# Graph layer and expert layers on one Trainium2 core: own products added by VectorE out of PSUM, the bias by a product, another order between sort and layer 0, blocks growing by one tile

## Chip, cores, metric

The kernel runs on one core of one Trainium2 chip (trn2). The metric is the device time of one execution in microseconds (us). Lower is better.

## What is computed

Nodes: 6250 rows x of 256 values. Edges: 100,000, each with `src`, `dst` and a weight, handed over in the order of `dst`. LN is a layer norm without factors. The reference does four steps; each adds its result to x:

```python
# layer 0, graph
h = LN(x) @ weight_l
x = x + segment_sum(edge_weight * h[dst], src) + bias_l + LN(x) @ weight_r + bias_r
# layer 0, eight dense experts e, hidden width 256, all applied to all rows
n = LN(x); w = softmax(n @ Wr + br)
h = relu(bn1(n @ W1[e] + b1[e])); h = relu(bn2(h @ W2[e] + b2[e]))
x = x + sum_e w[e] * (h @ Wo[e] + bo[e])
# layer 1, graph: sums over dst, gathers of src
x = x + segment_sum(edge_weight * (LN(x) @ weight)[src], dst) + bias
# layer 1, 32 experts, hidden width 64, one of them for each row (argmax)
x = x + relu(relu(LN(x) @ W1[i] + b1[i]) @ W2[i] + b2[i])
```

## The kernel before

The nodes are 49 tiles of 128 rows (`NT`), and x stays in SBUF as `X`. An aggregation works on columns of 128 edges: GpSimd (POOL) gathers 128 rows from DRAM by an indirect DMA (`gather`, L201, 12 buffers), ScalarE (ACT) and VectorE (DVE) weight them in two parts (`weighted`: `m`, L230 and L231), VectorE makes one-hot matrices of the edges' places in the tile (`one_hots`, L222), and TensorE (PE) multiplies both into `acc` (L701 in layer 0). A tile has 18 columns in layer 0 (`EW`).

**Sort.** Layer 0 sums by `src`, but the edges come by `dst`. So the kernel sorts them on the chip, in 25 groups (`NG`) of 32 columns of 128 edges. `count_group` (from L448) counts how many edges of a group go to each tile: `hot` (L454), `four`, `mine`, the count products on TensorE (L464 to L474), `start` and `total` by ScalarE. `settle_group` (L479) carries the counts on: `ZJ` (L482), `wrap` (L484), `base_of` (L486), `full_of` (L488), and `sizes` on POOL (L489). `place_group` (L491) finds the place of each edge: `same` (L497), `picked`, `pos`, `over`, `place_b` (L521), `to` (L523), and ScalarE's `loads` (L502); 32 products `put` (L530) bring the edges there; ScalarE copies them out (`there`, L533), and five POOL operations (L535 to L539) add them into the table `Z`.

Between these stand, in each group, the layer norm and the dense products of two node tiles: `center0` (L541: statistics, `std` with a Sqrt on ScalarE, the centred `xn`) and `products0` (L559): `xn` is transposed, `nT` copied (L341), `ph` = products by [weight_l | weight_r], 512 wide (L570), ScalarE's `hs` = `ph` times 1/std (L571). Half of `hs` goes to `h0` in DRAM (L574, SP's queue); POOL adds the other half to `X` (L572) and then the bias (L573). The loop is L577 to L592. After it stand a check of the counts (L595 to L610).

**Layer 0.** `edges0` (L662) reads columns of edges (`idx`, `dl`, `w`) for the tiles of a block out of `ZJ` and `Z`: per two tiles a comparison (L671), two products (L675) and two reductions (L677), then small operations (L678 to L686). The weights are loaded by DMAs that ACT's queue issues (L638 to L649); VectorE and ScalarE make `scale` and `shift` of the batch norms (L652 to L660). A block is one to four tiles; `ramp` (L358) gives the sizes: 1, 1, 2, 3, nine times 4, 3, 3. `begin0` (L712) normalizes a block, makes its gates and adds the experts' biases; `hidden0` (L742; products L748, ScalarE L751) makes a hidden layer of one expert; `outs0` (L755; products L760, VectorE L762) multiplies by Wo and adds into `X`; `end0` (L765) writes the rows that layer 1 gathers to `h1`.

The order is written by hand in the main loop (L883 to L936): block by block, expert by expert. `aheads` (L374) plans how many columns are issued between two steps: in block b, the first 12 of 16 steps bring the columns of block b+1, the last 4 a quarter of block b+2's. `begin0` of the next block stands after expert 5. `edges0` of block b+2 stands at expert 0 of block b. `small1` (L779), `early_columns` (L809) and `missing` (L820) prepare layer 1. A scheduler of the framework (Tile) orders the instructions of each engine from this program by priorities and may bring an instruction forward; each engine then runs its own list in order.

Layer 1 (`columns1`, L236; `begin1` and what follows, experts' products L984 to L1000) is touched only in the type of `dl_c`.

## Time and profile before

| | us |
|---|---|
| median of five runs | 2898.52 (2897.63 to 2903.07) |
| profiled execution | 2898.38 |
| its span in the trace | 2896.6 |
| mean granted TensorE clock | 0.975 |
| sort: last `to` (L523) begins | 377.8 |
| first gather of layer 0 (L201) begins | 396.3 |
| first hidden product (L748) begins | 440.9 |
| blocks 1, 2, 3, 4, 5 begin (first L748) | 471.4, 521.2, 595.6, 694.4, 805.5 |
| block 7 begins | 1015.7 |
| gather 432 (the last of tile 24) begins | 1006.9 |

Busy time over the span, from the page:

| engine | us | share |
|---|---|---|
| PE | 2676.5 | 92% |
| DVE | 2012.8 | 69% |
| POOL | 1929.5 | 67% |
| PEld (weight loads, beside PE) | 1746.4 | 60% |
| ACT | 1625.3 | 56% |

A share is a mean over stages with different limits, so the stages are looked at one by one. The page also cuts the span into 40 slices and gives each engine's busy tenths in each. A row of a timeline is: start and duration in us, engine, line, operation, output<-inputs by the program's names, shapes, the number of operations joined in the row, and in brackets how long the engine stood idle before it and what released it. A row of windows is: stretch, its length, the busy time of each engine with the number of operations, then the granted TensorE clock, the DMA engines' busy share and GB/s. In a row for one source line, three durations stand for the least, the median and the longest, in ns.

The longest idle time of the costliest groups belongs to gathers and what they feed; "idle before" is followed by what ended it:

```profile
L201 POOL DMA_INDIRECT g<-h,idx x882 | 903.3, 1024 | 392.5 <-DVE m L231 175.4
```

`<-DVE m L231` means that a gather waited for its buffer, which came free when L231 had weighted the column 12 before.

### The profile page before, as it was taken

What the parts mean: (1) busy time and instruction counts of PE and PEld (TensorE: products, weight loads), DVE (VectorE), ACT (ScalarE), POOL (GpSimd) and SP (SyncE); (2) the same over time, 40 slices, a digit from 0 to 9 for tenths busy, and PEclk for the clock granted to TensorE, in tenths of its full rate; (3) what the DMA queues carried; (4) which work ended last, traced back from release to release, by engine and by line L of the source; (5) the groups of instructions that cost most, each with busy time, mean ns of one, the idle gap of its engine ahead of it and who ended that gap; (6) DMA issues with size and microseconds to landing.
All of it is one profiled execution on the core that took longest, in us unless ns stands there. A gap on an engine that the chain in (4) does not pass through costs nothing.

```text
span 2896.6 us, 37030 instructions
## 1 busy us (share of the span) xinstructions
PE 2676.5 (92%) x10336; PEld 1746.4 (60%) x10336; DVE 2012.8 (69%) x4917; ACT 1625.3 (56%) x3790; POOL 1929.5 (67%) x1932
## 2 busy tenths in 40 slices
PE   5888848889999999999999998779999999999998
PEld 2444427666566666666666665556666666666666
DVE  8999977778768767666666556666666666666630
ACT  6777737555555555555555545455555555555532
POOL 4666667777766676766675527677777777777720
PEclk9999968999999999999999999899999999999999
DMA  4000043333333333333332214333333333333310
GB/s 150 19 19 19 19 144 96 99 100 102 93 99 95 91 101 95 92 100 97 90 103 83 79 39 141 101 106 100 106 108 109 107 108 101 109 106 108 109 46 12
DMA packets 123140, 260.73 MB, mean 90 GB/s; under 512 B 32236, under 2 KB 68904, under 8 KB 122920
## 3 DMA queue, kind: packets, MB, share of 16 engines
q0 software_dynamic: 79872, 218.21, 26.4%
q1 hardware_dynamic: 31672, 32.42, 3.4%
q10 hardware_dynamic: 11376, 7.60, 0.9%
q8 instruction: 85, 1.39, 0.2%
q14 instruction: 135, 1.11, 0.1%
HBM read 238.87 MB, written 19.25 MB: 89 GB/s over the span
## 4 chain that ended last, share of the span: by engine, by line
PE 63%; DMA 8%; DVE 6%; issue 4%; ACT 3%; POOL 1%; ACTq 0%; DVEq 0%; POOLq 0%
PE ph L748 19%; PE py L760 10%; PE py L1000 9%; PE ph L984 9%; PE acc L701 6%; DMA g<-h,src_c 4%; PE acc L277 4%; DMA g<-h,idx 3%; DVE m L231 2%; ACT m L230 2%; PE ph L214 1%; POOL g L201 1%; PE ph L987 1%; PE tr L340 1%; PE pl L957 1%
## 5 line engine op out<-in xcount | busy, mean ns | idle before, releaser
L201 POOL DMA_INDIRECT g<-h,idx x882 | 903.3, 1024 | 392.5 <-DVE m L231 175.4
L201 POOL DMA_INDIRECT g<-h,src_c x718 | 728.6, 1015 | 228.8 <-issue 102.7
L230 ACT ACTIVATE m<-g,w 128x256 fp32r<-128x256 f32 x882 | 394.7, 500 | 259.6 <-PE acc L701 138.3
L751 ACT ACTIVATE hT<-ph,shift,scale 128x512 f32<-128x512 f32 (+3 forms) x480 | 329.2, 696 | 315.7 <-PE ph L748 313.9
L230 ACT ACTIVATE m<-g,val_c 128x256 fp32r<-128x256 f32 x718 | 349.3, 503 | 277.8 <-PE acc L277 132.2
L231 DVE SCALAR_TENSOR_TENSOR m<-g,val_c,m 128x256 fp32r<-128x256 f32 x718 | 336.6, 482 | 214.2 <-ACT m L230 209.7
L231 DVE SCALAR_TENSOR_TENSOR m<-g,w,m 128x256 fp32r<-128x256 f32 x882 | 397.2, 476 | 42.6 <-ACT m L230 41.9
L748 PE MATMUL ph<-nT,w 128*128 128x512 f32 (+3 forms) x960 | 373.1, 524 | 25.0 <-ACT hT L751 24.9
L760 PE MATMUL py<-wo,hT 128*128 128x256 f32 x1568 | 380.6, 386 | 15.3 <-DVE X L762 11.3
L1000 PE MATMUL py<-w,hm 128*128 128x256 f32 x1568 | 384.9, 383 | 4.1 <-ACT hm L989 4.1
L701 PE MATMUL acc<-m,s 128*128 128x512 f32 x882 | 341.5, 490 | 37.8 <-DVE scale L657 24.7
L984 PE MATMUL ph<-nT,w 128*128 128x512 f32 (+2 forms) x832 | 376.1, 573 | 0.0
L748 PE MATMUL ph<-hT,w 128*128 128x512 f32 (+3 forms) x960 | 368.2, 518 | 0.5 <-ACT hT L751 0.5
L760 PEld LDWEIGHTS py<-wo,hT 128*128 128x128 f32 x1568 | 293.4, 192 | 82.5 <-DVE X L762 27.5
L277 PE MATMUL acc<-m,s 128*128 128x512 f32 x782 | 332.1, 499 | 1.7 <-DVE m L231 1.7
L1000 PEld LDWEIGHTS py<-w,hm 128*128 128x128 f32 x1568 | 290.3, 192 | 54.2 <-ACT hm L989 6.2
L222 DVE TENSOR_TENSOR s<-col,dl 128x384 fp32r<-128x384 f32 x294 | 161.3, 551 | 186.2 <-PE acc L701 183.8
L748 PEld LDWEIGHTS ph<-nT,w 128*128 128x128 f32 x960 | 175.5, 195 | 174.1 <-issue 118.3
L989 ACT ACTIVATE hm<-ph,b 128x512 f32<-128x512 f32 (+2 forms) x208 | 136.8, 659 | 198.7 <-PE ph L987 198.3
L748 PEld LDWEIGHTS ph<-hT,w 128*128 128x128 f32 x960 | 175.8, 193 | 119.2 <-issue 88.5
L701 PEld LDWEIGHTS acc<-m,s 128*128 128x128 f32 x882 | 169.4, 195 | 109.8 <-issue 48.8
L984 PEld LDWEIGHTS ph<-nT,w 128*128 128x128 f32 x832 | 157.3, 191 | 102.0 <-issue 81.6
(248 smaller groups left out, 3358.1 us busy)
## 6 DMA issues: line engine op xcount, KB each, us to landing
g<-h,idx POOLq DMA_INDIRECT x882, 2.8
g<-h,src_c POOLq DMA_INDIRECT x718, 2.8
h<-hs SPq DMA_DIRECT2D x25, 256.0 KB, 2.1
X<-in_x_dram SPq DMA_DIRECT2D x12, 512.0 KB, 9.4
out_dram<-o SPq DMA_DIRECT2D x11, 512.0 KB, 3.4
h<-hs SPq DMA_DIRECT2D x9, 512.0 KB, 3.1
w<-in_L_ffn_W_dram ACTq DMA_DIRECT2D x2, 2048.0 KB, 11.3
wo<-in_L_ffn_Wo_dram ACTq DMA_DIRECT2D x1, 2048.0 KB, 19.9
```

Source lines behind the costliest of these rows:

```text
L201: nc.gpsimd.indirect_dma_start(out=g, out_offset=None, in_=h, in_offset=bass.IndirectOffsetOnAxis(ap=idx, axis=0))
L222: nc.vector.tensor_tensor(s[:, :n], col[:, None, :].to_broadcast([P, n, P]), dl[:, j:j + n, None].to_broadcast([P, n, P]), OP.is_equal)
L230: nc.scalar.activation(m[:, 0, :], g, AF.Copy, scale=w)
L231: nc.vector.scalar_tensor_tensor(m[:, 1, :], g, w, m[:, 0, :], op0=OP.mult, op1=OP.subtract)
L277: nc.tensor.matmul(acc, s[:, (j - js.start) % SJ, :], m, start=opens, stop=done)
L701: nc.tensor.matmul(acc, s[:, j % SJ, :], m, start=(j == 0), stop=(j == EW - 1))
L748: nc.tensor.matmul(ph[:, :nw], (w1, w2)[layer][:, e, k, m * P:(m + 1) * P], src[:, k, :nw], start=(k == 0), stop=(k == 1))
L751: nc.scalar.activation(hT[:, m, :nw], ph[:, :nw], AF.Relu, bias=shift[:, layer, c:c + 1], scale=scale[:, layer, c:c + 1])
L760: nc.tensor.matmul(py, hT[:, k, j * P:(j + 1) * P], wo[:, e, k, :], start=(k == 0), stop=(k == 1))
L984: nc.tensor.matmul(ph[:, :nw], w1f[:, k, c * P:(c + 1) * P], nT[:, k, :nw], start=(k == 0), stop=False)
L989: nc.scalar.activation(hm[:, :nw], ph[:, :nw], AF.Relu, bias=b1[:, c:c + 1])
L1000: nc.tensor.matmul(py[:, j, :], now[:, cols], w2f[:, c, :], start=False, stop=(c == NC1 - 1), skip_group_check=True)
```

## The change

1. `products0` adds the own products to `X` by one VectorE operation out of PSUM; the two POOL adds go, and `hs` is half as wide. The statistics become `stats0`, done a group earlier than `center0`.
2. The bias is cut into three bf16 pieces at the start (on POOL), and a product of 128x256 adds it into `acc` in each tile of layer 0.
3. The last group's `to` is made in two halves, its five adds to `Z` are VectorE's, and the check of the counts is issued after `to`. `tc.issue_after(x)` puts the instructions in its body behind instruction x in the scheduler's order.
4. Between the sort and layer 0, `edges0` of block 0 stands first; the loads of weights are issued by SP behind it, `edges0` of block 1 after them, that of block 2 after half of the first tile's columns. From block 1 on, `edges0` of block b+2 is behind the newest operation of `outs0`; `small1`, `early_columns` and parts of `missing` too. In block 0, the first columns stand behind the block's norm and gates.
5. The blocks of layer 0 grow as 1, 1, 1, 1, 2, 2, 2, 3, 3, 3, six times 4, 3, 3: 18 in place of 15.
6. `dl_c` is bf16.

```diff
     nc.scalar.dma_start(wlr[:, :, 1, :], a["L0_gnn_weight_r"].rearrange("(k p) d -> p k d", p=P))
-    bias0 = across("L0_gnn_bias_l", early)
-    bias0r = across("L0_gnn_bias_r", early)
+    bias0 = across("L0_gnn_bias_l", prep)
+    bias0r = across("L0_gnn_bias_r", prep)
     nc.gpsimd.tensor_add(bias0, bias0, bias0r)
+    bias0_b = const.tile([P, D], BF, name="bias0_b")
+    nc.gpsimd.memset(bias0_b, 0.0)
+    ones_b = const.tile([P, P], BF, name="ones_b")
+    nc.gpsimd.memset(ones_b, 0.0)
+    for i in range(3):
+        own = slice(32 * i, 32 * i + 1)
+        nc.gpsimd.memset(ones_b[own, :], 1.0)
+        for _ in range(i):
+            nc.gpsimd.tensor_copy(bias0_b[own, :], bias0[own, :])
+            nc.gpsimd.tensor_sub(bias0[own, :], bias0[own, :], bias0_b[own, :])
+        nc.gpsimd.tensor_copy(bias0_b[own, :], bias0[own, :])
...
-    ramp = [1, 1, 2, 3] + [NB] * 9 + [3, 3]
+    ramp = [1] * 4 + [2] * 3 + [3] * 3 + [NB] * 6 + [3, 3]
...
         to = early.tile([P, CB, P, 4], BF, tag="to", name="to", bufs=2)
-        nc.vector.tensor_tensor(to, place_b[:, :, None, :].to_broadcast([P, CB, P, 4]),
-                                which_q[:, None, :, :].to_broadcast([P, CB, P, 4]), OP.is_equal)
+        final = g == NG - 1
+        step = CB // 2 if final else CB
+        for b in range(0, CB, step):
+            bs = slice(b, b + step)
+            placed = nc.vector.tensor_tensor(to[:, bs], place_b[:, bs, None, :].to_broadcast([P, step, P, 4]),
+                                             which_q[:, None, :, :].to_broadcast([P, step, P, 4]), OP.is_equal)
...
         some = early.tile([P, 2, NT], F32, tag="some", name="some", bufs=2)
-        nc.gpsimd.tensor_add(there[:, 0], there[:, 0], there[:, 1])
...
-    def center0(tiles):
+        eng = nc.vector if final else nc.gpsimd
+        eng.tensor_add(there[:, 0], there[:, 0], there[:, 1])
...
+        return placed
+    def stats0(tiles):
...
         nc.vector.tensor_scalar(std[:, :n], mv[:, :n, 1], LN_EPS, None, op0=OP.add)
-        shift = work.tile([P, NB], F32, tag="shift", name="shift")
+        shift = work.tile([P, NB], F32, tag="shift", name="shift", bufs=3)
         nc.scalar.activation(std[:, :n], std[:, :n], AF.Sqrt)
+        return tiles, std, shift
+    def center0(tiles, std, shift):
+        n = len(tiles)
+        rstd = work.tile([P, NB], F32, tag="rstd0", name="rstd0")
+        nc.vector.reciprocal(rstd[:, :n], std[:, :n])
             nc.scalar.activation(xn[:, j, :], X[:, t, :], AF.Identity, bias=shift[:, j:j + 1])
-        return tiles, xn, std
-    def products0(tiles, xn, std):
+        return tiles, xn, rstd
+    def products0(tiles, xn, rstd):
         n = len(tiles)
-        rstd = work.tile([P, NB], F32, tag="rstd0", name="rstd0")
-        nc.vector.reciprocal(rstd[:, :n], std[:, :n])
-        hs = early.tile([P, 2, 2, D], F32, tag="hs", name="hs", bufs=2)
+        hs = early.tile([P, 2, D], F32, tag="hs", name="hs", bufs=2)
                 nc.tensor.matmul(ph, nT[:, k, :], wlr[:, k], start=(k == 0), stop=(k == 1))
-            nc.scalar.activation(hs[:, j], ph, AF.Copy, scale=rstd[:, j:j + 1])
-            nc.gpsimd.tensor_add(X[:, t, :], X[:, t, :], hs[:, j, 1, :])
-            nc.gpsimd.tensor_add(X[:, t, :], X[:, t, :], bias0)
-        nc.sync.dma_start(h0[tiles[0] * P:(tiles[0] + n) * P, :].rearrange("(t p) d -> p t d", p=P), hs[:, :n, 0, :])
+            nc.scalar.activation(hs[:, j], ph[:, 0, :], AF.Copy, scale=rstd[:, j:j + 1])
+            nc.vector.scalar_tensor_tensor(X[:, t, :], ph[:, 1, :], rstd[:, j:j + 1], X[:, t, :],
+                                           op0=OP.mult, op1=OP.add)
+        nc.sync.dma_start(h0[tiles[0] * P:(tiles[0] + n) * P, :].rearrange("(t p) d -> p t d", p=P), hs[:, :n, :])
     counted = count_group(0)
-    centered = center0(pairs[0])
+    measured = stats0(pairs[0])
+    centered = center0(*measured)
+    measured = stats0(pairs[1])
         products0(*tiles0)
-        place_group(g, *now[:2])
+        placed = place_group(g, *now[:2])
         if g + 1 < NG:
-            centered = center0(pairs[g + 1])
+            centered = center0(*measured)
+            if g + 2 < NG:
+                measured = stats0(pairs[g + 2])
...
     most = early.tile([P, 2], F32, name="most")
-    nc.vector.tensor_reduce(most[:, 0:1], sizes.rearrange("p t g -> p (t g)"), AX.X, OP.max)
...
+    with tc.issue_after(placed.ins):
+        nc.vector.tensor_reduce(most[:, 0:1], sizes.rearrange("p t g -> p (t g)"), AX.X, OP.max)
...
             tc.tile_pool(name="psum_y0", bufs=1, space=bass.MemoryType.PSUM) as psum_y:
-        wr = wp.tile([P, 2, NX0], F32, name="wr")
-        nc.scalar.dma_start(wr, a["L0_ffn_Wr"].rearrange("(k p) e -> p k e", p=P))
...
-        bn = wp.tile([P, 2, 5, 2 * NX0], F32, name="bn")
-        nc.scalar.dma_start(bn, a["bn"])
-        wo = wo_pool.tile([P, NX0, 2, D], F32, name="wo")
-        for w, name in ((w1, "L0_ffn_W1"), (w2, "L0_ffn_W2"), (wo, "L0_ffn_Wo")):
-            nc.scalar.dma_start(w.rearrange("p e k h -> p (e k) h"), a[name].rearrange("e (k p) h -> p (e k) h", p=P))
...
             dl = wp.tile([P, NB, EW], F32, tag="dl", name="dl", bufs=3)
-            nc.vector.tensor_copy(dl[:, :n], bothi[:, :n])
+            told.append(nc.vector.tensor_copy(dl[:, :n], bothi[:, :n]))
         nblk = len(blocks0)
-        edges = [edges0(blocks0[0]), edges0(blocks0[1])]
+        told = []
+        edges = [edges0(blocks0[0])]
+        behind = ExitStack()
+        behind.enter_context(tc.issue_after(told[0].ins))
+        wr = wp.tile([P, 2, NX0], F32, name="wr")
+        nc.sync.dma_start(wr, a["L0_ffn_Wr"].rearrange("(k p) e -> p k e", p=P))
+        bn = wp.tile([P, 2, 5, 2 * NX0], F32, name="bn")
+        nc.sync.dma_start(bn, a["bn"])
+        wo = wo_pool.tile([P, NX0, 2, D], F32, name="wo")
+        for w, name in ((w1, "L0_ffn_W1"), (w2, "L0_ffn_W2"), (wo, "L0_ffn_Wo")):
+            nc.sync.dma_start(w.rearrange("p e k h -> p (e k) h"), a[name].rearrange("e (k p) h -> p (e k) h", p=P))
+        bo = wp.tile([P, D], F32, name="bo")
+        nc.vector.memset(bo, 0.0)
+        nc.sync.dma_start(bo[:NX0, :], a["L0_ffn_bo"])
+        gT = wp.tile([P, NB * P], F32, name="gT")
+        nc.vector.memset(gT, 0.0)
...
+        edges.append(edges0(blocks0[1]))
+        behind.close()
...
                         nc.tensor.matmul(acc, s[:, j % SJ, :], m, start=(j == 0), stop=(j == EW - 1))
+                        if j == 0:
+                            nc.tensor.matmul(acc[:, 0, :], ones_b, bias0_b, start=False, stop=False,
+                                             skip_group_check=True)
...
         plans[-1] = [cum[-1] + (NE - tail + CS // 2 + 3) * max(0, u + 1 - head) / (2 * NX0 - head) for u in range(2 * NX0)]
+        sums.upto(cum[0] // 2)
+        with tc.issue_after(newest["rest"].ins):
+            edges.append(edges0(blocks0[2]))
+        normed = [newest[k] for k in ("xn", "nT", "gates")]
+        def columns(b, e, half):
+            with ExitStack() as behind:
+                for ins in normed if b == 0 and e < 2 else ():
+                    behind.enter_context(tc.issue_after(ins.ins))
+                sums.upto(plans[b][2 * e + half])
             for e in range(NX0):
-                if e == 0 and b + 2 < nblk:
-                    edges.append(edges0(blocks0[b + 2]))
+                if e == 0 and 0 < b < nblk - 2:
+                    with tc.issue_after(newest["out"].ins):
+                        edges.append(edges0(blocks0[b + 2]))
                 if b == nblk - 3 and e == 3:
-                    small1()
-                    early_columns()
+                    with tc.issue_after(newest["out"].ins):
+                        small1()
+                        early_columns()
                 if final and e >= 5:
-                    next(fill)
-                sums.upto(plans[b][2 * e])
+                    with tc.issue_after(newest["out"].ins):
+                        next(fill)
+                columns(b, e, 0)
```

## The prediction

> **What bounds the kernel now.** I read the 40 slices of the page first, then the busy times by stage, then timelines of one sort group, of the sort's end and of the first blocks of layer 0.
>
> ```profile
> PE   5888848889999999999999998779999999999998
> DVE  8999977778768767666666556666666666666630
> PEclk9999968999999999999999999899999999999999
> ```
>
> One digit is 72.4 us. Up to slice 5 (362 us, the sort) VectorE is the full engine; then TensorE is, except in slices 5 to 8 (the step into layer 0 and its small blocks) and around 1750 to 1900. The change touches the sort and layer 0's beginning, so these two are costed.
>
> Busy time of every engine in 50 us of the sort (columns: stretch, length, PE, PEld, DVE, ACT, POOL, clock, DMA share, GB/s):
>
> ```profile
> 150.00:200.00 50.00, 43.95 (x190) 22.17 (x191) 50.00 (x109) 41.18 (x153) 33.55 (x34) 1.00 0.07 21
> ```
>
> VectorE has no gap, TensorE has 6.05 us: 1.7 us in each group of 14.34 us (from the starts of `to`, L523: 20 groups lie between 63.55 and 350.34). Part of VectorE's time is not work. Timeline of one group (start, duration, engine, line):
>
> ```profile
> 350.34 2.27 DVE L523 TENSOR_TENSOR to<-place_b,which_q 128x4096 bf16<-128x4096 bf16 x1
> 350.55 2.66 POOL L572 TENSOR_TENSOR X<-X,hs 128x256 f32<-128x256 f32 x1 [0.50 <-ACT hs L571]
> 352.67 5.14 PE L530 MATMUL put<-loads,to 128*128 128x245 bf16 x22
> 353.28 0.73 POOL L573 TENSOR_TENSOR X<-X,L_gnn_bias_l_b 128x256 f32<-128x256 f32 x1
> 353.33 0.73 DVE L484 TENSOR_SCALAR wrap<-total 128x49 f32<-128x49 f32 x1
> 353.98 0.80 POOL L572 TENSOR_TENSOR X<-X,hs 128x256 f32<-128x256 f32 x1
> 353.98 0.20 DVE L488 SCALAR_TENSOR_TENSOR full_of<-total,full_of 128x49 f32<-128x49 f32 x1
> 354.17 0.68 DVE L486 TENSOR_TENSOR base_of<-total,wrap 128x49 bf16<-128x49 f32 x1
> ```
>
> L484, L486 and L488 have the same 49 columns; L488 takes 0.20, the other two 0.7, and each of those ends with the POOL add beside it. The POOL add is stretched likewise (2.66 beside `to`, 0.73 alone).
>
> **The change, part by part.**
>
> *Own products and bias out of POOL.* It removes the 98 POOL adds (L572, L573). Over the 25 groups the least and median durations are: L484 174 and 728 ns, L486 199 and 673, L497 398 and 877, L482 404 and 751. Taking L482 in full, the excess is 0.55 + 0.47 + 0.48 + 0.35 = 1.85 us a group; I take 1.75, because POOL keeps five adds of its own (L535 to L539) and one subtraction. Added are two `scalar_tensor_tensor` a group, 128x256, PSUM and SBUF in. The nearest row has this very shape:
>
> ```profile
> L762 DVE SCALAR_TENSOR_TENSOR X<-py,gate,X x392: 464/478/486, 450.6 to 1821.9; 128x256 f32<-128x256 f32 x196
> ```
>
> It takes 478 ns alone, and L231's six in a row took 2.46 us, 0.41 each; so +0.8 to +0.96 a group. Net on VectorE: -0.8 to -0.95 us of 14.34.
>
> [...]
>
> But VectorE's gain is only paid until TensorE and ScalarE set the period. In the group above ScalarE's `nT` (350.37) waits behind its `hs` (349.78), the four products L570 start at 350.80 and end at 352.78, and `put` starts at 352.67 while `to` had ended at 352.61. How long TensorE waits for `to` (us, times, longest), from 63 to 350 us:
>
> ```profile
> PEld L530 <- DVE to L523: 13.9, 20, 1.5
> ```
>
> That is 0.70 a group, the most that a faster VectorE takes off this wait. Following the chain `put`, `there`, two `loads`, `start`, `nT`, `nT`, products, `put` in the changed kernel's built order (its `hs` is half as wide, its Sqrt is one group earlier) I get 0.33 a group. I take the middle of the two, 0.5: 23 groups x 0.5 = **-11.5 us**; bounds 0 and 23 x 0.95 = -22.
>
> The additions also make VectorE wait for `ph`. In the built order they stand on both sides of `four` (L458 of before), right behind `hot`; queued behind them are `mine`, and so the counts, `start` and ScalarE's `loads`. `ph` was ready at 352.78, `hot` started at 354.76, so 2 us cover the wait; without them it costs what it exceeds them, on VectorE itself.
>
> *Bias in three bf16 pieces.* In the built order 11 of the new POOL operations stand before the iota of `which_t` (12.82). No row has an operation of one partition; the bounds are 0 and the 0.80 of L192's add, 0 to 8.8 us in all. Nearest in size are the adds of 49 columns (0.27 to 0.30); I take 0.4 each, 4.4 us. POOL makes `ahead` at 15.04 + 0.22, VectorE uses it at 17.25 (L439), so 2.0 us are covered: **+2.5 us**, 0 to +7.
>
> The products of 128x256 bf16 on TensorE: 49, priced by L998 (the same shape, 109 ns from start to start). The first 19 or so are in the stretch that the gathers set (below); 30 x 0.11 = **+3.3 us**.
>
> *The end of the sort, and layer 0's beginning.* After the last `place_b`:
>
> ```profile
> 376.25 0.29 DVE L521 TENSOR_TENSOR place_b<-pos,over 128x32 bf16<-128x32 f32 x1
> 376.46 1.42 DVE L596 TENSOR_REDUCE most<-sizes 128x1 f32<-128x1225 f32 x1
> 377.80 2.27 DVE L523 TENSOR_TENSOR to<-place_b,which_q 128x4096 bf16<-128x4096 bf16 x1
> 380.13 7.39 PE L530 MATMUL put<-loads,to 128*128 128x245 bf16 x32 [3.04 <-DVE to L523]
> 396.31 1.39 POOL L201 DMA_INDIRECT g<-h,idx  x1 [6.80 <-DVE at_m L827]
> ```
>
> L596 moves behind `to` (-1.4) and `to` comes in halves (-1.1). Between the last Z (389.5) and the first gather VectorE did two memsets (0.75), small operations of L785 to L827 and half of block 1's `edges0`, now all later: about -2.3. First gather about 391.5, -4.8. POOL's five Z adds on VectorE instead are equal (49 columns, 0.2 to 0.3 each).
>
> What follows is set by the gathers until TensorE has a full load. TensorE busy, by block (length, busy):
>
> ```profile
> 471.30:521.10 49.80, 38.92 (x213) 0.89 0.34 98
> 595.50:694.30 98.80, 87.17 (x323) 0.97 0.36 99
> 805.40:910.50 105.10, 105.01 (x367) 1.00 0.34 96
> ```
>
> ```profile
> 497.40:548.20 50.80, 39.81 (x36) 0.90 0.35 97
> 953.20:1006.80 53.60, 35.83 (x36) 1.00 0.32 90
> ```
>
> The second fence is POOL in line L201 alone: 36 gathers take 50 us early (1.38 each) whatever TensorE does. The smaller blocks cost TensorE nothing by their size: the pitch of L748 is 112, 216, 322 and 429 ns for one to four tiles. So the place to compare is one where both have done 19 tiles and aggregated 24 (432 gathers): before, block 7's start at 1015.7, gather 432 having left at 1006.9. After, 391.5 + 431 x 1.379 = 986. But `edges0` of block b+2 now stands behind the previous block's outs. In the built order the indices of blocks 3 and 4 (gathers 54 and 72) are written only after all 54, and after 71, earlier columns have been weighted; before, gather 72's came after 37. The queue runs dry twice, for about 8.5 and 10 us: the way from a last gather to its weighted column, and `edges0` of two tiles (L671 to L683, 5 to 7 us). 986 + 18.5 = 1004.5, and the same state is passed some 5 us later, 1009.7: **-6 us** with the -4.8 in it. Bounds: without stops -29 (nearly TensorE's own limit), with pitch 1.44 or longer stops +10.
>
> *Three more blocks* (18 for 15): three more begin0/end0, among them ACT table loads of 1.28 us. They lie beside products of the running block, which TensorE has queued. I cost them 0; uncovered, two loads a block, +7.7 us. The weights' loads on SP instead of ACT take away 8 us in which ACT issues DMAs (391.4 to 399.5), but the wait that this frees is before the first tile's gathers are in, so no more than the gathers give. `small1`, `early_columns` and `missing` move late; from 1725 to 1900 TensorE has gaps of 25 us, so 0, +-3. Layer 1 is unchanged but for `dl_c` in bf16; VectorE has slack there: 0.
>
> **Sum**, against the profiled execution's own 2898.38 (span 2896.6 and 1.8 around it; the median, 2898.52, is 0.1 from it): +2.5 - 11.5 - 6 + 3.3 = -11.7, so **2887 us**.
>
> **Rivals.**
>
> *B, VectorE is the sort's only bound and the gathers don't stop.* For: no gap in VectorE's row, and `to` ended 0.06 before `put` began. Against: the 0.33 of the chain, and the order of the columns 54 and 72. +2.5 - 22 - 29 + 3.3: 2853 us.
>
> *C, the sort keeps its period*, since `nT`, products and `put` follow each other through ScalarE. For: TensorE's 1.7 us of gaps a group are less than half waits for `to`. +2.5 + 0 - 6 + 3.3: 2898 us.
>
> *D, slower: the gather stream stops at block heads.* Place: POOL's queue at each head of blocks 3 to 8, where `edges0` waits for the previous block's outs. Two stops are counted; price 10 us each. A third brings 2897, from the fourth on it is slower: 2907 us. For: gathers are what slices 5 to 8 wait for. Against: from block 5 on, the built order has 17 or more gathers written ahead, 23 us.
>
> *E, the change doesn't free VectorE*: what remains on POOL holds L484, L486 and L497 as before, and the two additions come on top, 24 x 0.85 = +20: 2913 us.
>
> **How the numbers follow.** A difference of 0.2% (5.8 us; 2892.7 to 2904.3) is about what a measurement of this kernel can tell from none. Forecast 0.54 (its own range 2874 to 2900: faster 0.38, same 0.16); B 0.20, faster; C 0.11 (same 0.09, faster 0.02); D 0.11 (slower 0.10, same 0.01); E 0.04, slower. Faster 0.60, same 0.26, slower 0.14. The range, 2858 to 2907, leaves out the far end of B (about 0.1) and E with the worse half of D (0.1); it takes in the bounds of the sort and the gathers one at a time.
>
> **What would show it.** Period between `to`s about 13.8 us; L484 and L486 at 0.2; if they stay at 0.7, E. VectorE with gaps in the sort means that the chain is the bound; none and a period of 13.4 means B. First gather near 382. POOL idle twice near gathers 54 and 72; more often, D. The first hidden product near 420, 24 tiles aggregated near 995. TensorE in layer 0's blocks of four at 105 us plus 0.44. The forecast is wrong if layer 1 changes by more than 3 us, or if any block after the tenth has TensorE gaps.

## The result and the profile after

The changed kernel is **slower**: median 2910.91 us (2902.22 to 2915.62, 24 runs) against 2901.93 us (45 runs of the kernel before), ratio 1.0030 (1.0024 to 1.0035). A second measurement (chip number 11 on record) gave 1.0036 (1.0023 to 1.0048). The forecast was 2887, 0.4% faster, in a range of 2858 to 2907. The profiled execution took 2901.92 us (span 2900.1), 3.5 more than that of before; it is the fastest of the changed kernel's runs, and so is the traced one of the second measurement (2902.21); experiment 10 comes back to this. The medians of the kernel before differ between measurements (2896 to 2902, and far more in seven runs, experiment 11), so versions are compared by their ratio to the kernel before, run beside them on the same chip.

The page's slices of the changed kernel:

```profile
PE   4888858899899899999999998889999999999998
DVE  7999966778777677687677656666666666666630
PEclk9999969999999999999999999889999999999999
```

The digits hardly differ: TensorE is a tenth fuller in slices 6 and 9 and a tenth emptier in 1 and 11, and VectorE's digits at the start (90% or more) hide the gaps that it now has there. Where the time went, by the starts of the same instructions in both traces (us; gathers are counted from 0, so gather 432 is the first behind the 24th tile, and the last of that tile left at 1004.9 before):

| | before | after | difference |
|---|---|---|---|
| first `to` | 31.3 | 38.4 | +7.1 |
| fifth `to` | 92.9 | 103.5 | +10.6 |
| 24th `to` | 364.5 | 367.8 | +3.3 |
| first gather | 396.3 | 398.2 | +1.9 |
| first hidden product | 440.9 | 432.4 | -8.5 |
| gather 72 | 497.5 | 515.7 | +18.2 |
| 19 tiles done (block 7; block 10) | 1015.7 | 1017.0 | +1.3 |
| last block of layer 0 | 1716.4 | 1718.8 | +2.4 |
| end of span | 2896.6 | 2900.1 | +3.5 |

So there is no one place. The sort loses 10.6 us at its start and wins 7.3 back; the first block starts sooner; then 16 us are lost from the first gather to gather 72, and given back up to the 19th tile.

**The sort.** Windows of 150 to 200 us, then three of VectorE's groups in 150 to 300 us:

```profile
150.00:200.00 50.00, 44.93 (x207) 23.47 (x206) 47.71 (x118) 37.40 (x145) 16.24 (x20) 1.00 0.07 22
```

```profile
L598 DVE SCALAR_TENSOR_TENSOR X<-ph,rstd,X 128x256 f32<-128x256 f32 x22 | 10.6, 480 | 6.2 <-ACT hs L597 6.2
L500 DVE TENSOR_TENSOR base_of<-total,wrap 128x49 bf16<-128x49 f32 x10 | 2.1, 207 | 0.2 <-issue 0.2
L498 DVE TENSOR_SCALAR wrap<-total 128x49 f32<-128x49 f32 x10 | 1.8, 182 | 0.0
```

`wrap` and `base_of` are down from 0.73 and 0.67 to 0.18 and 0.21 us, the new operation takes 0.48, VectorE (third busy time) has gaps, and the period is 13.90 us for 14.30. TensorE's wait for `to`, 13.9 us in 20 waits before, no longer appears between 63 and 350 us. That is the step as forecast: the chain of TensorE and ScalarE takes over.

**Its start.** Timeline, then VectorE's waits from 20 to 80 us (total, times, longest):

```profile
19.34 0.55 POOL L444 IOTA which_t<- 128x196 bf16 x1
19.92 0.98 DVE L468 TENSOR_TENSOR hot<-tb,which_t 128x1568 bf16<-128x1568 bf16 x1 [2.86 <-POOL which_t L444]
23.48 0.18 DVE L453 TENSOR_SCALAR ahead<-ahead 128x64 bf16<-128x64 bf16 x1 [2.58 <-POOL ahead L451]
```

```profile
DVE X L598 <- ACT hs L597: 7.7, 5, 4.4
```

`which_t` begins 6.5 us later than before (12.82) and `ahead` 8.2 later, and VectorE waits for both. Then VectorE waits in the first groups for the products that it is to add, up to 4.4 us each: the second `to` begins 18.5 us after the first (13.8 before).

**Its end.** The last Z addition, the first `at` of `edges0`, and the first gather:

```profile
389.64 0.25 DVE L557 TENSOR_TENSOR Z<-there,some 128x49 f32<-128x49 f32 x1
393.79 0.40 DVE L677 TENSOR_TENSOR at<-ZJ,place 128x468 bf16<-128x468 bf16 x1 [3.61 <-DVEq L308]
398.17 1.21 POOL L213 DMA_INDIRECT g<-h,idx  x1 [15.62 <-DVE bo L710]
```

`DVEq L308` is VectorE's own sequencer at the branch (`tc.If`) that ends the sort. Its rows, before and after (three durations in ns, then the first start):

```profile
L294 DVEq COMPARE_BRANCH  x2: 63/68/72, 382.9 to 2889.6; - x2
```

```profile
L308 DVEq COMPARE_BRANCH  x2: 63/68/72, 390.3 to 2892.6; - x2
```

Before, nothing of VectorE's stood late ahead of that branch, so it was reached at 382.9, while `put` ran (380.1 to 387.5); now five additions stand there, and the branch comes after them, at 390.3: 3.6 us in which VectorE does nothing.

**The gathers.** POOL in the gathers' line alone, at three places, after and before:

```profile
468.00:480.00 12.00, 1.15 (x2) 0.86 0.10 23
502.00:516.00 14.00, 1.28 (x2) 1.00 0.13 20
851.00:862.00 11.00, 1.84 (x2) 1.00 0.05 17
```

```profile
468.00:480.00 12.00, 9.56 (x9) 1.00 0.32 86
502.00:516.00 14.00, 10.95 (x11) 0.87 0.30 90
851.00:862.00 11.00, 7.53 (x9) 1.00 0.33 97
```

Two gathers in 11 to 14 us, where the kernel before has 9 to 11 (the longest time between two of its gathers up to gather 432 is 3.4 us): the stream stops ahead of gather 54 (11.5 us), 72 (13.6) and 321 (10.5). The first two wait for indices. The third waits for a buffer: for 10 us (850.6 to 860.5) VectorE has no weighted column, only the four-tile `edges0`, norms and outs.

### The profile page after: what moved, and what is told of

It is laid out like the page before. It is cut to its first block, busy times and chain, and to the rows that moved or that the text cites. A ratio compares the mean times of both kernels' runs of the same rounds, so it can differ in the third digit from the quotient of the medians.

```text
span 2900.1 us, 38036 instructions
## 1 busy us (share of the span) xinstructions
PE 2688.6 (93%) x10769; PEld 1797.4 (62%) x10769; DVE 2002.8 (69%) x5030; ACT 1649.4 (57%) x3904; POOL 1830.1 (63%) x1843
## 4 chain that ended last, share of the span: by engine, by line
PE 62%; DMA 8%; issue 5%; DVE 4%; ACT 3%; POOL 1%; ACTq 0%; POOLq 0%; DVEq 0%
PE ph L788 20%; PE py L800 10%; PE ph L1039 8%; PE py L1055 8%; PE acc L738 6%; DMA g<-h,src_c 5%; PE acc L291 4%; DMA g<-h,idx 3%; DVE m L243 2%; ACT m L242 2%; POOL g L213 1%; PE ph L1042 1%; PE ph L226 1%; PE tr L354 1%; DMA g<-h,idx_e 1%
## 5 line engine op out<-in xcount | busy, mean ns | idle before, releaser
L791 ACT ACTIVATE hT<-ph,shift,scale 128x512 f32<-128x512 f32 (+3 forms) x576 | 360.1, 637 | 300.1 <-PE ph L788 295.9
L243 DVE SCALAR_TENSOR_TENSOR m<-g,val_c,m 128x256 fp32r<-128x256 f32 x718 | 336.8, 483 | 208.7 <-ACT m L242 204.7
L243 DVE SCALAR_TENSOR_TENSOR m<-g,w,m 128x256 fp32r<-128x256 f32 x882 | 398.9, 476 | 70.9 <-ACT m L242 69.2
L788 PE MATMUL ph<-nT,w 128*128 128x512 f32 (+3 forms) x1152 | 384.9, 465 | 24.7 <-ACT hT L791 24.7
L1055 PE MATMUL py<-w,hm 128*128 128x256 f32 x1568 | 382.9, 382 | 3.0 <-ACT hm L1044 3.0
L738 PE MATMUL acc<-m,s 128*128 128x512 f32 x882 | 358.5, 497 | 29.0 <-DVE m L243 28.5
L788 PE MATMUL ph<-hT,w 128*128 128x512 f32 (+3 forms) x1152 | 379.9, 461 | 3.0 <-ACT hT L791 3.0
L800 PEld LDWEIGHTS py<-wo,hT 128*128 128x128 f32 x1568 | 292.6, 191 | 76.9 <-DVE X L802 15.1
L291 PE MATMUL acc<-m,s 128*128 128x512 f32 x782 | 332.6, 499 | 1.7 <-DVE m L243 1.7
L788 PEld LDWEIGHTS ph<-nT,w 128*128 128x128 f32 x1152 | 203.5, 194 | 147.5 <-issue 72.0
L788 PEld LDWEIGHTS ph<-hT,w 128*128 128x128 f32 x1152 | 205.1, 193 | 97.2 <-issue 48.5
L1039 PEld LDWEIGHTS ph<-nT,w 128*128 128x128 f32 x832 | 158.3, 192 | 102.4 <-issue 82.1
```

The lines of the kernel that those rows point to most:

```text
L243: newest["rest"] = nc.vector.scalar_tensor_tensor(m[:, 1, :], g, w, m[:, 0, :], op0=OP.mult, op1=OP.subtract)
L291: nc.tensor.matmul(acc, s[:, (j - js.start) % SJ, :], m, start=opens, stop=done)
L738: nc.tensor.matmul(acc, s[:, j % SJ, :], m, start=(j == 0), stop=(j == EW - 1))
L788: nc.tensor.matmul(ph[:, :nw], (w1, w2)[layer][:, e, k, m * P:(m + 1) * P], src[:, k, :nw], start=(k == 0), stop=(k == 1))
L791: nc.scalar.activation(hT[:, m, :nw], ph[:, :nw], AF.Relu, bias=shift[:, layer, c:c + 1], scale=scale[:, layer, c:c + 1])
L800: nc.tensor.matmul(py, hT[:, k, j * P:(j + 1) * P], wo[:, e, k, :], start=(k == 0), stop=(k == 1))
```

## The experiments

Ratios to the kernel before on the same chip, with 95% intervals. "Changed" stands at 1.0030 and 1.0036. Seven more runs, which fell on another level of times, have their ratios in experiment 11.

| run | edit | ratio |
|---|---|---|
| e1_bias_late | changed, bias made late | 1.0008 (0.9999 to 1.0018) |
| e2_five_on_pool | changed, Z additions on POOL | 1.0016 (1.0006 to 1.0026) |
| e3_edges_free | changed, `edges0` free | 1.0072 (1.0056 to 1.0087) |
| e4_old_blocks | changed, old blocks | 0.9987 (0.9976 to 0.9999) |
| f2_three_undone | e1, e2 and e4 together | 0.9974 (0.9964 to 0.9983) |
| f3_edges_half_block | changed, `edges0` earlier | 0.9970 (0.9958 to 0.9982) |
| f4_blocks_alone | before, new blocks | 1.0072 (1.0059 to 1.0085) |
| g1_pool_adds_back | changed, POOL's adds back | 0.9998 (0.9989 to 1.0007) |
| g2_new_blocks_mended | e1, e2 and f3 together | **0.9943** (0.9930 to 0.9956) |
| g3_old_blocks_mended | g2 with old blocks | 0.9971 (0.9961 to 0.9981) |

**1. The bias's pieces.** The add, the pieces and the ones go behind the memset of ZJ on POOL:

```diff
-    nc.gpsimd.tensor_add(bias0, bias0, bias0r)
-    bias0_b = const.tile([P, D], BF, name="bias0_b")
...
     nc.gpsimd.memset(ZJ[:, :, NG], 0.0)
+    nc.gpsimd.tensor_add(bias0, bias0, bias0r)
+    bias0_b = const.tile([P, D], BF, name="bias0_b")
...
```

> The changed kernel with one edit: the bias's add, pieces and ones are made on POOL behind the memset of ZJ, so behind which_t, which_q, ahead and base_of. Theory 1 (the eleven small POOL operations ahead of which_t cost the sort's beginning 7 to 11 us): first `to` back near 31 to 33 us (38.4 in the changed kernel, 31.3 before), the fifth near 94 to 96 (103.5), period 13.9 kept, first gather near 389, and 7 to 9 us less than the changed kernel in the end. Rival (the beginning is caught up anyway, since statistics and DMAs of X set it): fifth `to` still near 101 or later, time within 3 us of the changed kernel.

First `to` 34.1 (38.4), fifth 100.7 (103.5), first gather 395.3. VectorE's waits from 20 to 80 us:

```profile
DVE X L598 <- ACT hs L597: 8.4, 4, 5.5
```

Of the 10.6 us lost up to the fifth `to` only 2.8 are these operations: the theory held for a quarter of it. Part of the rest is the wait for `hs`. Run 8, which has neither the pieces nor this wait, passes the fifth `to` at 96.7, still 3.8 behind the kernel before; so pieces made late and wait together cost the 4.0 between the two runs, and the 3.8 stay open.

By the medians the end is 6 us better, but the traces don't show this as the earlier start: 19 tiles are done at 1017.3 (1017.0) and the last block of layer 0 begins at 1719.0 (1718.8), since the stops ahead of gathers 54 and 72 are now 12.7 and 15.1 us long (11.5 and 13.6). The 4.4 us between the two traced executions arise in layer 1, which the edit doesn't touch.

**2. The last five additions.**

```diff
-        eng = nc.vector if final else nc.gpsimd
+        eng = nc.gpsimd
```

> The changed kernel with the last group's five additions to Z back on POOL. Theory 2 (VectorE's instructions ahead of the branch at the end of the sort hold back the branch itself, 3.6 us, which was hidden beside `put` before): VectorE's idle time ahead of the first `at` falls from 3.6 to under 1 us although the five take 1.4 on POOL against 0.9 on VectorE; first gather 3 us earlier, about 395. Rival (the wait is not the branch but something behind it, such as instruction loading that starts only at the branch's end): the 3.6 us stay and the first gather is at 398 to 399. In the end either is worth 0 to 3 us.

The same three places of the timeline as above:

```profile
389.58 0.30 POOL L557 TENSOR_TENSOR Z<-there,some 128x49 f32<-128x49 f32 x1
389.91 0.40 DVE L677 TENSOR_TENSOR at<-ZJ,place 128x468 bf16<-128x468 bf16 x1 [5.08 <-POOL Z L557]
394.29 1.21 POOL L213 DMA_INDIRECT g<-h,idx  x1 [4.41 <-DVE bo L710]
```

`at` follows the end of the last addition by 0.03 us in place of 3.90. VectorE waits 5.1 us, but for the data: its last operation ahead of the branch ended at 384.8, and the branch is hidden again. First gather 394.3, 3.9 earlier; the last block of layer 0 begins 2.6 earlier (1716.2).

**3. `edges0` free to move.**

```diff
                 if e == 0 and 0 < b < nblk - 2:
-                    with tc.issue_after(newest["out"].ins):
-                        edges.append(edges0(blocks0[b + 2]))
+                    edges.append(edges0(blocks0[b + 2]))
```

> The changed kernel with edges0 of block b+2 no longer behind the previous block's outs, free to be brought forward as before the change. Theory 3 (the gather stream runs dry because edges0 stands behind the outs: 11.5 us ahead of gather 54, 13.6 ahead of 72, 10.5 ahead of 321): the three stops are under 4 us each, gather 432 leaves near 985 to 990 in place of 1010.6, block 10 begins near 993 to 1000 in place of 1017.0, and the end is 15 to 22 us earlier than the changed kernel's, so 8 to 12 us faster than before. Rival (the stops only take the place of waits that TensorE's work would bring anyway, TensorE being nearly full from block 4 on): gather 432 near 1003 or later, the end within 5 us of the changed kernel.

This **missed**: 12 us slower than the changed kernel. The product of `edges0` (L681) on VectorE up to 520 us, changed kernel (from 398) and this one (from 399):

```profile
L681 DVE TENSOR_TENSOR there<-at,Z 128x450 f32<-128x450 bf16 (+1 forms) x8 | 5.8, 725 | 0.0
```

```profile
L681 DVE TENSOR_TENSOR there<-at,Z 128x900 f32<-128x900 bf16 (+1 forms) x17 | 14.7, 866 | 0.1
```

Freed, `edges0` of several later blocks is brought ahead of the columns that are wanted now. VectorE's idle time ahead of its weighted columns (L243) halves, from 21.1 to 11.1 us, block 0 takes 44.3 us (31.0), and the stream stops at gather 74 for 11.0 us, because VectorE weights no column from 499.4 to 512.7. So `edges0` can stand too early as well as too late.

**4. Old blocks in the changed kernel.** `ramp = [1, 1, 2, 3] + [NB] * 9 + [3, 3]`.

> The changed kernel with the old blocks (1, 1, 2, 3, nine of 4, 3, 3). Theory 3 (the stops come from edges0's place, the block sizes by themselves are worth little): fewer heads early, so fewer stops, but each behind an edges0 of more tiles; 19 tiles done at 1010 to 1020, the end within 4 us of the changed kernel. Rival (smaller blocks are what gives TensorE work while gathers are behind): 19 tiles done at 1025 or later and the end 8 us or more slower than the changed kernel.

Better than both expected: 12 us faster than the changed kernel by the medians, 9.0 between the traced executions. No stop at 54 or 72 (gather 72 leaves at 494.8), three later ones of 6.4 to 8.8 us, 19 tiles done at 1007.9.

**5. `edges0` half a block earlier, in a fixed place.** Run first among the seven of experiment 11 (e5), then again (f3):

```diff
-                if e == 0 and 0 < b < nblk - 2:
+                if e == NX0 // 2 and b + 3 < nblk:
                     with tc.issue_after(newest["out"].ins):
-                        edges.append(edges0(blocks0[b + 2]))
+                        edges.append(edges0(blocks0[b + 3]))
```

> The changed kernel, edges0 half a block earlier: in block b, at expert 4, edges0 of block b+3 behind the newest outs (expert 3), in place of edges0 of block b+2 at expert 0 behind the last outs of block b-1. So the order is fixed, as in the changed kernel, but gather 54's indices stand behind 37 weighted columns (54 in the changed kernel), gather 72's behind 59 (71 to 72). Theory 3 (the stops come from how late edges0 stands, and freeing it entirely was slow because VectorE then did several blocks' edges0 ahead of weighted columns): no stop above 5 us at 54, 72 and 321, gather 432 near 985 to 995, 19 tiles done at 998 to 1006, 10 to 18 us faster than the changed kernel. Rival (edges0's cost on VectorE in the small blocks is the loss, wherever it stands): the first tiles get later instead, and the end stays within 5 us of the changed kernel.

> As the run with edges0 half a block earlier in the changed kernel, again for a chip like the first. Theory 3 (the stops of the gathers come from how late edges0 stands): no stop above 5 us at gathers 54, 72 and 321, gather 432 near 985 to 995, 10 to 18 us faster than the changed kernel. Rival (edges0's cost on VectorE in the small blocks is the loss, wherever it stands): within 5 us of the changed kernel.

In f3 no gap up to gather 432 is over 5.4 us; gather 72 leaves at 496.8 (515.7), gather 432 at 1000.9 (1010.6; 985 to 995 was expected), 19 tiles are done at 1005.0 (1017.0). Windows of 396 to 1016 us, all engines, changed kernel and f3:

```profile
396.00:1016.00 620.00, 556.54 (x2507) 424.23 (x2508) 453.35 (x1183) 394.77 (x834) 444.70 (x436) 0.95 0.36 102
```

```profile
396.00:1016.00 620.00, 571.01 (x2552) 437.04 (x2553) 469.56 (x1218) 399.65 (x850) 462.99 (x444) 0.93 0.38 104
```

TensorE has 14.5 us more to do in the same stretch, at a lower mean clock. One place in the order, 0.0066 of the time, 19 us by the medians and 12.6 between the traced executions, 12.0 of them there at 19 tiles: the largest single effect found, and theory 3 is shown by it.

**6. New blocks in the kernel before.**

> The kernel before with the new blocks alone (18, growing by one tile). Theory 3b (small blocks have more edges0, norms and ends per tile ahead of the weighted columns on VectorE, and the scheduler brings edges0 forward): block 0 or 1 is 8 us or more longer than need be, as in the run with edges0 freed, and the end is 8 to 16 us slower than before. Rival (small blocks give TensorE work sooner, and only the order of the changed kernel spoils it): 4 to 10 us faster than before.

> As the run of the kernel before with the new blocks alone, again for a chip like the first. Theory 3b (more edges0, norms and ends per tile ahead of the weighted columns on VectorE): 8 to 16 us slower than before. Rival (small blocks give TensorE work sooner, the order of the changed kernel spoils it): 4 to 10 us faster than before.

f4 is 21 us slower than before, more than expected. Gather 72 leaves at 504.8, after the one stop (9.0 us), and 19 tiles are done at 1036.0, 20 us later than before and close to run 3 (1033.8). What loses the rest between is not shown.

**7. Own products alone,** in the kernel before (the pieces made late; statistics, order and blocks of before):

```diff
-            nc.scalar.activation(hs[:, j], ph, AF.Copy, scale=rstd[:, j:j + 1])
-            nc.gpsimd.tensor_add(X[:, t, :], X[:, t, :], hs[:, j, 1, :])
-            nc.gpsimd.tensor_add(X[:, t, :], X[:, t, :], bias0)
+            nc.scalar.activation(hs[:, j], ph[:, 0, :], AF.Copy, scale=rstd[:, j:j + 1])
+            nc.vector.scalar_tensor_tensor(X[:, t, :], ph[:, 1, :], rstd[:, j:j + 1], X[:, t, :],
+                                           op0=OP.mult, op1=OP.add)
```

> The kernel before with the own products on VectorE out of PSUM and the bias by a product (made on POOL behind ZJ's memset, dl_c bf16 for the room); statistics, order and blocks as before. Theory 4 (the period of a sort's group falls to the chain of TensorE and ScalarE, 13.9 us, and that is all there is in it): period 13.9 to 14.1, sort ends 5 to 9 us earlier, +2 to 3 us in layer 0 by the bias's products: 0.997 to 0.999 of before. Rival (the statistics done a group earlier are what shortened the chain): period 14.2 to 14.5, time within 3 us of before or slower by the bias.

It is one of the seven of experiment 11, so only its sort is read; e7, another of them, has the period of before, 14.30. Here it is **16.44 us**. The granted clock is lower in this sort (0.90 from 150 to 200 us, 1.00 in e7), but its products take as long as e7's (`ph` 592 ns, `put` 405), so it is not the clock. The first addition of a group, and VectorE's waits from 150 to 350 us:

```profile
212.16 0.48 DVE L583 SCALAR_TENSOR_TENSOR X<-ph,rstd,X 128x256 f32<-128x256 f32 x1 [3.31 <-ACT hs L582]
```

```profile
DVE X L583 <- ACT hs L582: 39.4, 12, 3.3
```

With the statistics in their old place the products come late, the addition waits 3.3 us in each group, and `to` stands behind it. Neither expected period held: without `stats0` a group earlier the part loses 2.1 us a group. Run 8 has the early statistics alone, and they win nothing either; only the two together shorten the period.

**8. POOL's adds back, all else as changed.** The 512-wide `hs` and the two adds come back; pieces and products of the bias go.

> The changed kernel with its first part undone: the own products and the bias are added to X by POOL again out of a 512-wide hs, no bias pieces, no bias products; statistics a group early, order, edges0 and blocks as in the changed kernel. Theory 4 (VectorE is freed from POOL's adds by that part, and the chain of TensorE and ScalarE then holds 13.9 us): the operations on 49 columns (wrap, base_of) are back at 0.7 us and the period is 14.2 to 14.5 us; but the first `to` is back at 31 to 33 us and the second period at 14 us, since neither the eleven POOL operations nor VectorE's wait for ph in the first groups is there; sort ends within 3 us of the changed kernel, so the part is worth nothing in sum. Rival (the early statistics alone shorten the period): 13.9 us or less with POOL's adds too, and the sort ends 8 us or more earlier than in the changed kernel.

Windows of 150 to 200 us, and two groups of VectorE in 150 to 300:

```profile
150.00:200.00 50.00, 43.75 (x193) 22.08 (x191) 50.00 (x106) 40.58 (x150) 26.36 (x37) 1.00 0.05 17
```

```profile
L487 DVE TENSOR_SCALAR wrap<-total 128x49 f32<-128x49 f32 x10 | 6.7, 674 | 0.0
L489 DVE TENSOR_TENSOR base_of<-total,wrap 128x49 bf16<-128x49 f32 x10 | 6.7, 673 | 0.0
```

VectorE is full again, the 49 columns cost 0.67 (0.18 and 0.21 in the changed kernel), the period is 14.3; but the first `to` is at 33.2 and the second 13.8 later. First gather 397.9, with the part 398.2: in the sort it nets **nothing**. And in layer 0 it costs the bias's products. One block of four tiles, changed kernel and g1:

```profile
1121.20:1226.10 104.90, 104.90 (x369) 65.81 (x368) 77.29 (x195) 59.73 (x115) 74.67 (x70) 1.00 0.33 93
```

```profile
1122.80:1227.30 104.50, 104.50 (x365) 65.77 (x364) 77.49 (x195) 59.67 (x115) 74.89 (x71) 1.00 0.34 94
```

0.40 us for four products, as forecast (0.44).

By the medians the part costs more: 0.9998 without it, 1.0030 and 1.0036 with it, 9 us or more, of which the two traced executions show 1.5 (spans 2898.6 and 2900.1). The difference is not located; see experiment 10.

**9. Combinations.**

> The changed kernel with three parts undone together: bias made on POOL behind ZJ's memset, the last five additions to Z on POOL, the old blocks. If the three costs are separate (6 us, 4 us and 12 us by the ratios 1.0008, 1.0016 and 0.9987 against 1.0030), this is 1.0030 - 0.0022 - 0.0014 - 0.0043 = 0.995 of before, 14 us faster. Rival (the earlier start is absorbed, since the gathers of the first 24 tiles set the time): 0.9975 to 0.999.

> As the run with three parts undone together (bias made late on POOL, the last five additions to Z on POOL, old blocks), again for a chip like the first. Separate costs: 0.995 of before, 14 us faster. Rival (absorbed by the gathers of the first tiles): 0.9975 to 0.999.

> The changed kernel with the new blocks, edges0 half a block earlier, the bias made late on POOL and the last five additions to Z on POOL. If the earlier sort's end (about 6 us: first gather 390.4 in the run with three parts undone) passes through to layer 0 now that gathers don't stop: 0.9970 - 0.0022 = 0.994 to 0.9955 of before, 13 to 17 us faster, the fastest of all. Rival (absorbed, as in the run with three parts undone, where 0.995 was expected and 0.9974 measured): 0.9965 to 0.9975.

> The same with the old blocks (1, 1, 2, 3, nine of 4, 3, 3), edges0 half a block earlier. Tells what the block sizes are worth once edges0 stands early. If small blocks give TensorE work sooner: 4 to 8 us slower than the run with the new blocks, 0.9965 to 0.998. Rival (block sizes are worth nothing by themselves): within 2 us of it.

With old blocks part of the earlier sort is absorbed: the first gather comes at 390.4 against 397.3 of e4, 6.9 us earlier, the last block of layer 0 begins 5.0 earlier, and the ratios (0.9974 against 0.9987, 4 us) have overlapping intervals. With new blocks and `edges0` half a block earlier it is paid: for a first gather at 391.1 against 397.8 of f3 the last block begins 6.9 earlier, and g2 against f3 is 0.0027, 8 us. g2 is the best version, 17 us faster than before (2880.00 against 2897.38). g3 against g2: once `edges0` stands rightly, the blocks that grow by one tile win 8 us; in the changed kernel they lost 12.

**10. The changed kernel again.**

> The changed kernel as it is, beside the three that follow on one chip, since the last four fell on a chip on which the kernel before takes 3286 us (2896 to 2902 elsewhere) and the granted clock is 0.93. Chip like the first: 1.003 of before (1.0024 to 1.0035 measured). Theory 5 (the changed kernel's loss in the medians beyond the 3.5 us of the two profiles is granted clock): clock 0.972 to 0.974 in its runs against 0.974 to 0.976 in those of before. Rival: equal clocks on both.

Ratio 1.0036, mean granted clock of its runs 0.9744 against 0.9752. Over all runs with a recorded clock: changed 0.9735 (26), before 0.9748 (29), 0.9752 (15), 0.9746 (23). The question is whether this explains why the medians differ by 9 us and the profiles by 3.5. It explains little. A straight line through the 26 runs of the changed kernel falls by about 1.0 us for each 0.001 of clock, lines through the three sets of the kernel before by 0.1, 1.0 and 1.7; by these slopes, an estimate, 0.0013 is worth 1 to 2 us. And the traced execution of f1, 2902.21 us at a clock of 0.974, is 5.8 to 12.6 us faster than its other four at 0.974 and 0.975. Why the changed kernel's usual execution takes 8 to 9 us more than its traced ones stays open, and with it why several edits gain more over it by the medians than by the traces.

**11. Another level of times.** Runs e5, e6, e7 and e8 (chip number 9 on record), h1 and h2 (12) and i1 (7) were taken where the kernel before takes 3225 to 3286 us at a granted clock of 0.93 to 0.94; in e5 and e7 TensorE is busy 84% of the span. It isn't one chip: under number 7 runs 1 to 4 had the kernel before at 2896. Where the time goes is seen in the same kernel at both levels, f4 and e7: the first gather of layer 0 leaves at 396.0 and 396.7, its last block begins at 1736.1 and 1909.8. So the sort takes as long, and what gathers takes longer; from 440 to 1000 us the DMA engines move 93 and 78 GB/s at a granted clock of 0.96 and 0.89. What sets the level is not shown. At it every version is slower than before: e5 1.0224, e6 1.0227, e7 1.0094, e8 1.0090. The three later ones:

> The changed kernel with edges0 half a block earlier, the last five additions to Z on POOL, and the own products and bias added by POOL as before the change (no bias pieces, no bias products). If that part costs 9 us wherever it stands (0.9998 without it, 1.0030 to 1.0036 with it): 0.991 to 0.993 of before, faster than the run with the bias made late by 2 us or more. Rival (its cost was the eleven POOL operations, which the late bias avoids, and VectorE's shorter sort pays the products): 0.9945 to 0.996.

> The run with the new blocks, edges0 half a block earlier, the bias late and the five additions on POOL once more, to stand beside the other on one chip: 0.9943 of before (0.9930 to 0.9956 measured).

> The mended kernel with POOL's adds once more, the last two runs having fallen on the chip on which the kernel before takes over 3200 us. Part costs 9 us wherever it stands: 0.991 to 0.993 of before. Rival (its cost was mostly the eleven POOL operations): 0.9945 to 0.996, against 0.9943 of the mended kernel with own products on VectorE.

h1 1.0287 (1.0262 to 1.0312), i1 1.0230 (1.0192 to 1.0267), h2 1.0207 (1.0181 to 1.0234): all three far from what was expected. Whether the own products are worth keeping in the mended kernel stays open: h2 is better than h1, on the same chip, by 0.008, but i1's interval overlaps h2's, and this level says little of the other.

## Why the prediction was wrong

- **Sum up to the first gather: wrong.** Forecast +2.5 - 11.5 - 4.8 = -13.8; measured +1.9. Between the two traced executions this is all of the error (forecast -11.7, measured +3.5). What failed is the account of the sort's two ends, where two waits had been put at nothing:
  - *"`ph` was ready at 352.78 ... so 2 us cover the wait"*: true in the steady state (0.6 a group), read from one group in the middle. In the first groups nothing covers it: up to 4.4 us in the changed kernel and 5.5 in run 1. Run 1 and run 8, with the wait and without, are 4.0 apart at the fifth `to`.
  - *The bias's pieces, +2.5*: 2.8 by run 1, so the size was about right, but not the way to it. `which_t` came 6.5 us later and `ahead` 8.2, first `to` +7.1. The add ahead of them was done 1.1 us later, the eleven took 0.5 us each, not 0.4, and of three more, which I had not counted, two stood between `which_t` and `ahead`.
  - Another 3.8 us of the 10.6 lost at the start are in run 8 too. The sum has no term for them, and their cause stays open.
  - *The end, -4.8*: -1.4 from the 24th `to` to the first gather. I priced the five additions on VectorE at nothing, by their durations, and did not see what they are ahead of: the branch, 3.6 us. With the additions on POOL (run 2) the same stretch is 4.6 us shorter than before.
- **The sort's period: right.** 0.40 a group for 0.5, and the mechanism (the chain takes over) with it; from the fifth to the 24th `to` -7.3. Rivals B (13.4), C (14.3) and E (0.7 kept) are out. (E's own terms sum to 2918, not 2913.) But own products and bias as a whole, forecast at +2.5 - 11.5 + 3.3, win nothing: run 8 undoes them and has its first gather 0.3 us earlier.
- **The gathers: right in sum, and a lucky one.** From first gather to 19 tiles -1.2 was forecast, -0.6 measured. The two stops came where the built order said, but 11.5 and 13.6 long for 8.5 and 10; a third (rival D) came at gather 321, not from missing indices but from VectorE's burst of `edges0`. From gather 72 to 306 the pitch was 1.35 us for 1.38. What the price hid is what stood there to be won: 19 us by run 5. It also hid that the two terms don't simply add: while the stops stand, a first gather 2.9 us earlier (run 1) brings 19 tiles no earlier; without them (g2 against f3), 6.7 bring 7.2.
- **The bias's products: right,** 0.40 us in a block of four.
- **"It takes 478 ns":** 480 (L598, mean from 150 to 300 us). The row of the same shape was a good price.
- **The range** failed for two reasons. The start and the end of the sort had bounds of a few us each; the traced execution, 2901.9, still lies inside. The medians lie 5.4 us beyond the two profiles' difference, and nothing here explains that.

## What to carry to other kernels

A steady state read from one group prices the steady state: first and last rounds of a pipeline need their own line. Here the new wait was 0.6 us a group in the steady state and up to 4.4 us in the first groups. When work is put on an engine, ask also what it stands ahead of there: a branch (3.6 us here), an iota (6.5 us later here), the next block's work. A step that feeds a queue can have two wrong places, as `edges0` had here: too late (the gathers stopped for up to 13.6 us) and too early (11.0 us in run 3, behind work for later blocks). Fix its place (half a block of lead won 19 us by the medians in run 5), and only then judge the block sizes.

## What the runs showed of the hardware

- The branch at the sort's end took 3.6 us between two operations of VectorE, 2.9 of them behind the compare (390.3 to 393.2). Where VectorE reached it early and then waited for data, the next operation followed the data by 0.03 us (run 2).
- Small POOL operations of one partition and 256 elements took 0.4 to 1.2 us at the start of the kernel, beside VectorE's work; 128 partitions of 256 columns took 0.72 at the least (L573 of before).
- The same kernel took 3225 to 3286 us in place of 2896 to 2902 in some measurements, one of them under a chip number that had shown 2896 within the hour, with a granted clock of 0.93 to 0.94 for 0.975, and the sign of several versions turned (f3 0.9970, e5, the same kernel, 1.0224). A gain of some tenths of a per cent in one measurement need not hold in another.
